# Reading half-filled maxima tiles early, one block's shift rows ahead of other transfers, and LayerNorm statistics joined on GpSimd: one Trainium2 kernel before and after

## The chip, the cores and the metric

The kernel runs on one core of one Trainium2 (trn2) chip. Five engines run their own instruction streams in order and meet through semaphores: PE (TensorE, matrix products), DVE (VectorE), ACT (ScalarE), POOL (GpSimd) and SP (SyncE, which here only issues transfers). The metric is device time in microseconds (us); 35758 instructions are in the trace of one execution.

## The reference, cut to what matters

Input x is (8, 1024, 256); 16 query heads of 16 columns share 4 key and value heads; scores are scaled by 1/16.

```python
n = layernorm(x)
q, k = rope(n @ Wq), rope(n @ Wk)          # 16 heads of q, 4 of k and v
v = n @ Wv
p = softmax(q @ k.T / sqrt(256))           # per head, over 1024 keys
x = x + layernorm((p @ v) @ Wo)
f = layernorm(x) @ (ternary(W) * alpha).T + bias
x = x + layernorm(f)
```

layernorm is (x - mean) / sqrt(var + 1e-5) over 256 columns, without weights.

## The kernel before, in words

**Units and blocks.** The batch is cut into 16 units of 512 queries (`NU`), a unit into 4 blocks (`G`): block i is 512 queries of 4 heads. For each block the score matrix is made twice. One pass (`max_scores`, matmul at L576) has queries on the partitions and 512 keys in the free dimension, and DVE reduces it to the row maximum over the keys (L590). The other (`exp_scores`, L628) has keys on the partitions, and ACT takes its exponential straight into the weights of the value product (L643, then `av_piece`, L663). The maximum reaches the second pass as two extra rows of the query operand `q_st`, which the matmul itself subtracts: DVE splits the maximum into a high and a low part (`shift_split`, L603 and L162, tile `mhl`), PE transposes it (`shift_rows`, L610, tile `pm`), ACT copies it out (L612, `mh`), and SP writes it into rows 48 and 49 of both halves of `q_st` by two transfers (L619). No exponential of a block can be started before its shift rows have landed.

**A maxima tile** (`sm`) is 128 x 2 x 512 fp32 in PSUM, two buffers (`ps_mx`). Two matmuls fill it, one per half (for blocks after the first: both halves of the 1024 keys for one group of rows), and one reduction over both halves (L590, `AX.XY`, 1024 elements to one) empties it. There are 1024 such tiles: 16 of block 0, which keeps its halves apart (`mx_half`, L586, joined at L588), and 1008 of the other blocks.

**The order of the work** is written out by hand for PE, DVE and ACT (`manual_schedule`). It goes by windows: `window` takes three scores of the second pass and, alternating with them, three maxima matmuls that run ahead (`maxima_by`: 40 to 48 matmuls ahead), then whatever `parts_of_step` has for that place (products, transposes, LayerNorm statistics of other units: `Project`, `Tail`), then the value products of a window two back (`av_windows`). A block of 32 scores is ten windows of three and one of two. Three is odd, so every second window of three ends with a maxima tile that is half filled; its second half is the first maxima matmul of the next window.

**GpSimd and SP** are not in that list after the first steps: a planner places their instructions. SP's one queue carries all transfers in the order the planner gives it: inputs, rotated queries out to DRAM and back into `q_st` (`q_to_dram`, L472; `stack_queries`, L542 and the constant rows L146), keys (`kt`, L430; `stack_keys`, L481), the shift rows and the tails' tensors.

**LayerNorm** (`ln_stats`): DVE takes `bn_stats` of each 128 x 256 tile (L237; for each half of the columns a count, a mean and a sum of squared deviations) and joins them by `bn_aggr` (L239); GpSimd adds the epsilon, takes the power -0.5 and negates the mean (L241 to L243).

**The start.** At step numbers below zero only maxima are made; exponentials of block 0 and the projection of units 1 and 2 run side by side. A list at L952 to L978 says which part of which projection comes at which step: `third("kt")` at the thirteenth entry, `stack_queries` of unit 1 at the nineteenth.

Of the kernel before, what the change touches and what calls it, by code (L numbers as in the profile page):

```python
# [8 lines left out]
F32 = mybir.dt.float32  # L9
F32R = mybir.dt.float32r  # L10
AF = mybir.ActivationFunctionType
ALU = mybir.AluOpType
AX = mybir.AxisListType
# [3 lines left out]
P = 128  # L17
# [4 lines left out]
UT = 4  # L22
UQ = UT * P
EPS = 1e-5
# [4 lines left out]
def kernel(  # L29
# [29 lines left out]
    nc = tc.nc  # L59
    B, S, D = x.shape  # L60
# [4 lines left out]
    NK = S // P  # L65
# [9 lines left out]
    small = ctx.enter_context(tc.tile_pool(name="small", bufs=4))  # L75
# [10 lines left out]
    def load_x(u, tag, bufs):  # L86
        b, half = divmod(u, UPB)
        t = xp.tile([P, UT, D], F32, tag=tag, name=f"{tag}_{u}", bufs=bufs)
        src = x[b, half * UQ : (half + 1) * UQ, :].rearrange("(t p) d -> p t d", p=P)
        for ts in (slice(0, 2), slice(2, 4)) if u == 0 else (slice(0, 4),):  # L90
            nc.sync.dma_start(out=t[:, ts, :], in_=src[:, ts, :])
        return t

    x_sb = {0: load_x(0, "x", 2)}
# [4 lines left out]
    mhalf = const.tile([P, 2], F32, name="mhalf")  # L99
# [7 lines left out]
    for src, lo, n in ((w_q, 0, D), (w_k, D, DK), (w_v, ROT, DK)):  # L107
        nc.sync.dma_start(
            out=wqkv[:, :, lo : lo + n], in_=src.rearrange("(c p) n -> p c n", p=P)
# [51 lines left out]
    def split_lo(eng, lo, src, hi):  # L161
        eng.tensor_tensor(lo, src, hi.bitcast(F32), ALU.subtract)  # L162
# [65 lines left out]
        nc.scalar.copy(wt, pt)  # L228


    def ln_stats(src):

        n = src.shape[1]
        mv = small.tile([P, 2, 2], F32, tag="mv", name="mv")[:, :n]
        st = small.tile([P, 2, 6], F32, tag="bnst", name="bnst")
        for t in range(n):
            nc.vector.bn_stats(st[:, t, :], src[:, t, :])  # L237
        for t in range(n):
            nc.vector.bn_aggr(mv[:, t, :], st[:, t, :])  # L239
        sc = small.tile([P, 2, 2], F32, tag="lnsc", name="lnsc")[:, :, :n]  # L240
        nc.gpsimd.tensor_scalar(sc[:, 1, :], mv[:, :, 1], EPS, 1.0, ALU.add, ALU.mult)  # L241
        nc.gpsimd.tensor_tensor(sc[:, 1, :], sc[:, 1, :], mhalf[:, :n], ALU.pow)  # L242
        nc.gpsimd.tensor_scalar(sc[:, 0, :], mv[:, :, 0], -1.0, 0.0, ALU.mult, ALU.add)  # L243
        return mv, sc
# [60 lines left out]
    class Project:  # L305
# [19 lines left out]
                    for p in range(2)  # L325
                ]

        def stats(self, p):
            self.sc[p] = ln_stats(x_sb[self.u][:, 2 * p : 2 * p + 2, :])

        def norm(self, p, eng=None):
            src = x_sb[self.u][:, 2 * p : 2 * p + 2, :]
# [6 lines left out]
            split_lo(eng or self.eng, self.xs[p][1], self.xn[p], self.xs[p][0])  # L339

        def begin(self, p):
            self.stats(p)
            self.norm(p)
            self.hi(p)
            self.lo(p)
# [203 lines left out]
    mx = {}  # L549

    def block_queries(i, r2=slice(None)):

        u, j = divmod(i, G)
        if u < NU - 1:
            return q_st[u % 2][:, j, r2, :]
        return q_st[u % 2][:, :, r2, j * P : (j + 1) * P]

    def max_scores(v):


        i, k = divmod(v // 2, 2 * NK)
        u, part = i // G, v % 2
        if i == 0:
            a, ch, t, r2 = 1 - part, k // NK, k // 2 % UT, k % 2
        else:
            a, ch, t, r2 = 1 - k % 2, part, k // 4, k // 2 % 2
        queries = block_queries(i, r2)
        queries = queries[:, t * P : (t + 1) * P] if u < NU - 1 else queries[:, t]
        if part == 0:
            sm[0] = ps_mx.tile([P, 2, 512], F32, tag="sm", name=f"sm_{i}_{k}")  # L570
            if k == 0:
                mx[i] = small.tile([P, 2, UT, 2], F32, tag="mx", name=f"mx_{i}")
            if k == 0 and i == 0:
                mx["half"] = small.tile([P, 2, 2, UT, 2], F32, tag="mx0", name="mx_half", bufs=1)
        rows = slice(64 * a, 64 * a + 64)
        nc.tensor.matmul(  # L576
            sm[0][:, part, :],
            queries[rows],
            k_st[(u // UPB) % 3][rows, r2, ch * 512 : (ch + 1) * 512],
            start=True,  # L580
            stop=True,
        )
        if part == 0:
            return
        if i == 0:
            nc.vector.tensor_reduce(mx["half"][:, ch, ::-1, t, r2], sm[0], AX.X, ALU.max)  # L586
            if k == 2 * NK - 1:
                nc.vector.tensor_tensor(mx[0], mx["half"][:, 0], mx["half"][:, 1], ALU.max)  # L588
        else:
            nc.vector.tensor_reduce(mx[i][:, a, t, r2 : r2 + 1], sm[0], AX.XY, ALU.max)  # L590
        if k == 2 * NK - 1:
            shift_split(i)
            due.append((v // 4 + (1 if i < 2 else 2), i))

    sm, mhl = {}, {}

    def shift_split(i):

        m = mx.pop(i)
        hl = mhl[i] = small.tile([P, 2, 2, 2 * UT], F32R, tag="mhl", name=f"mhl_{i}")  # L600
        order = "(r t)" if i // G < NU - 1 else "(t r)"
        hi, lo = (hl[:, :, l].rearrange(f"p a {order} -> p a t r", r=2) for l in range(2))
        nc.vector.tensor_copy(hi, m)  # L603
        split_lo(nc.vector, lo, m, hi)

    def shift_rows(i):

        hl = mhl.pop(i)
        pm = psum([8 * UT, P], f"pm_{i}", F32R)
        nc.tensor.transpose(pm, hl.rearrange("p a l x -> p (a l x)"), ident_r)  # L610
        mh = work.tile([8 * UT, P], F32, tag="mh", name=f"mh_{i}")
        nc.scalar.copy(mh, pm.bitcast(F32))  # L612
        n = 4 * UT
        for a in range(2):
            row = 64 * a + NROW
            dst = block_queries(i)[row : row + 2].bitcast(F32)
            if len(dst.shape) == 4:
                dst = dst.rearrange("l j c t -> l (j c) t")
            nc.sync.dma_start(out=dst, in_=mh[n * a : n * a + n, :])  # L619


    es, av_ps, av_sb, d_av = {}, {}, {}, {}
# [64 lines left out]
    class Tail:  # L687
# [85 lines left out]
            ln_apply(self.eng(p), self.on[p], self.x1[p], self.sc[p])  # L773

        def stats_a(self, p):
            self.sc[p] = ln_stats(self.a[p])
            self.add(p)

        def stats_x(self, p):
            self.sc[p] = ln_stats(self.x1[p])  # L780
            self.norm(p)
            self.split(p)

        def stats_f(self, p):
            self.sc[p] = ln_stats(self.a[p])
            self.end(p)

        def ffn(self, p):
# [157 lines left out]
    def second(name, *args):  # L946
        return lambda: getattr(projects[1], name)(*args)

    def third(name, *args):
        return lambda: getattr(projects[2], name)(*args)  # L950

    for k, fs in enumerate((  # L952
        [second("x", 1, 0), second("x", 1, 1), second("kv", 0)],
        [second("kv", 1), (pick, "q", 0, 0, 1), (pick, "q", 0, 1, 1), second("v"),
         second("rotate_k"), second("split_k")],
        [(pick, "q", 1, 0), (keep_warm, 1)],
        [(keep_warm, 3), second("k"), (keep_warm, 4), (pick, "k", 1, 0), (pick, "k", 1, 1),
         (keep_warm, 2)],
        [(pick, "q", 1, 1), second("q_product", 0), third("stats", 0),
         third("norm", 0, nc.scalar)],  # L960
        [second("q_product", 1), third("stats", 1), third("hi", 0, nc.scalar), third("lo", 0),
         (pick, "q", 2, 0)],
        [(pick, "q", 2, 1), third("norm", 1, nc.scalar), third("hi", 1, nc.scalar),
         third("lo", 1), (keep_warm, 3), (fill_constant_parts, 1)],
        [third("x", 0, 0), (pick, "q", 3, 0), (keep_warm, 3)],
        [third("x", 0, 1), (pick, "q", 3, 1), second("rotate_q", 0), (keep_warm, 2)],
        [third("x", 1, 0), third("x", 1, 1), second("split_q", 0)],
        [third("kv_and_dram"), second("rotate_q", 1)],
        [third("v"), second("split_q", 1), second("q_to_dram")],
        [third("kt")],  # L970
        [],
        [(fill_constant_parts, 2)],
        [],
        [third("q", 0)],
        [],
        [third("q", 1), (stack_queries, 1)],
        [third("q_to_dram")],
    )):  # L978
        for f in fs:
            at(k - START, *(f if isinstance(f, tuple) else (f,)))  # L980
# [46 lines left out]
    maxima = [0]  # L1027
# [24 lines left out]
    def window(i, s, size, late):  # L1052
        if done:
            av_out(done.pop())
        if late:
            for r2 in range(2):
                exp_two(s // 4, r2)
        else:
            end = min(maxima_by(s + size), 4 * NSTEP)
            for q in range(max(size, end - maxima[0])):  # L1060
                if q < size:
                    exp_one(s + q)
                if maxima[0] < end:
                    max_scores(maxima[0])
                    maxima[0] += 1
        behind.append((i, s, size))
        for n in range(s // 4, (s + size) // 4):
            parts_of_step(n)
        av_windows(1 if late else 2)
# [135 lines left out]
```

## Time and profile before

| | |
|---|---|
| time, median of 3 runs (lowest to highest) | 1734.97 us (1734.68 to 1735.65) |
| the profiled execution's own time | 1735.28 us |
| its span (first to last instruction) | 1733.1 us |
| busy PE / DVE / ACT / POOL | 92% / 81% / 73% / 48% of the span |
| mean granted TensorE clock | 0.983 of full speed |
| maxima reductions (L590) | 1008, 1218 ns each, 1190.5 us |
| exponentials (L643) | 2000, 602 ns each, 1055.9 us |

How to read it: a busy share says how full an engine is, not that it sets the time; matmuls overlap and are shown busy while they wait, so PE's 92% is no measure of its work. The rows of the waits name who waited for whom, with the total, the count and the longest. In the chain of work that ended last each step is followed back to what released it. A row of a group reads: line, engine, operation, out<-in with its shape, count | busy us, mean ns of one | idle time before it and who ended it.

### The profile page before, as it was taken

Reading aid. Unit: us, or ns where it says so; the run is one execution under the profiler, and the core shown is the slowest. Engines: PE = TensorE matmul, PEld = TensorE weight load, DVE = VectorE, ACT = ScalarE, POOL = GpSimd, SP = SyncE. Lnnn points to the kernel's source line nnn. Section 1 sums busy time; section 2 is a strip of 40 time slices with the busy share of each in tenths; the row PEclk is TensorE's granted clock in tenths of the full one; section 3 lists DMA queues with packets and bytes.
Section 4 is the critical chain, followed back from the end, with each engine's and each line's share of the span. In section 5 each row is a group of like instructions: output and inputs, shape, how many; then the busy total and the mean of one; then the engine's idle time right before and its main releaser. Section 6 shows DMA issues by size and latency. Waiting matters only on the chain.

```text
span 1733.1 us, 35758 instructions
## 1 busy us (share of the span) xinstructions
PE 1602.1 (92%) x14200; PEld 834.1 (48%) x14200; DVE 1398.1 (81%) x1752; ACT 1271.0 (73%) x2479; POOL 836.0 (48%) x1239
## 2 busy tenths in 40 slices
PE   7969999999999999999999999999999999999997
PEld 5534454444544445454454544545454544444444
DVE  6848778888788888878888788888978887888874
ACT  4637777777687777868777777877777786877775
POOL 5522447274453637346374644737455362333354
PEclk8879999999999999999999999999999999999999
DMA  4330424225151332515124151412414141140100
GB/s 131 66 78 32 83 73 87 63 76 97 41 101 43 82 82 61 104 39 98 51 74 96 54 102 46 90 58 78 84 48 95 45 87 51 33 82 32 40 14 25
DMA packets 86071, 117.88 MB, mean 68 GB/s; under 512 B 12089, under 2 KB 50809, under 8 KB 85753
## 3 DMA queue, kind: packets, MB, share of 16 engines
q1 hardware_dynamic: 85904, 115.60, 28.9%
q8 instruction: 112, 1.84, 0.5%
q14 instruction: 55, 0.44, 0.1%
HBM read 68.65 MB, written 45.88 MB: 66 GB/s over the span
## 4 chain that ended last, share of the span: by engine, by line
PE 34%; DVE 13%; POOL 4%; ACT 4%; issue 1%; DMA 1%; SPq 0%; POOLq 0%; ACTq 0%; DVEq 0%
PE av L663 13%; DVE mx L590 10%; PE se L628 10%; PE sm L576 4%; ACT e L643 3%; PE pa L283 2%; PE pf L283 1%; PE pq L283 1%; PE pt_ot L267 1%; DMA dq<-hlq 1%; DVE bnst L237 1%; PE pkv L283 1%; PE pt_xt L267 1%; POOL hlq L162 1%; DVE mhl L603 0%
## 5 line engine op out<-in xcount | busy, mean ns | idle before, releaser
L590 DVE TENSOR_REDUCE mx<-sm 128x1 f32<-128x1024 f32 x1008 | 1190.5, 1218 | 285.5 <-PE sm L576 242.2
L643 ACT ACTIVATE e<-se 128x512 f32<-128x512 f32 x2000 | 1055.9, 602 | 301.3 <-PE sm L576 238.5
L576 PE MATMUL sm<-k_st,q_st 64*128 64x512 f32 x2048 | 736.2, 449 | 45.7 <-DVE mx L590 41.8
L628 PE MATMUL se<-q_st,k_st 64*128 64x512 f32 x2048 | 685.8, 434 | 19.3 <-DMA q_st<-mh 18.3
L663 PE MATMUL av<-e,v_aug 128*32 128x256 f32 (+3 forms) x8096 | 591.7, 392 | 0.0
L628 PEld LDWEIGHTS se<-q_st,k_st 64*128 64x128 f32 x2048 | 330.8, 186 | 368.3 <-ACT e L643 217.3
L576 PEld LDWEIGHTS sm<-k_st,q_st 64*128 64x128 f32 x2048 | 324.5, 186 | 156.7 <-DVE mx L590 125.0
L663 PEld LDWEIGHTS av<-e,v_aug 128*32 128x32 f32 x8096 | 184.3, 109 | 192.6 <-issue 145.7
L241 POOL TENSOR_SCALAR lnsc<-mv 128x2 f32<-128x2 f32 (+1 forms) x134 | 25.8, 193 | 453.6 <-DVE mv L239 448.7
L737 POOL TENSOR_TENSOR xn<-xn,a 128x512 f32<-128x512 f32 x30 | 38.4, 1280 | 129.0 <-DMA a<-d_rec 115.1
L798 POOL TENSOR_TENSOR a<-a,bias_bc 128x512 f32<-128x512 f32 x30 | 39.0, 1300 | 117.2 <-ACT a L797 117.2
L242 POOL TENSOR_TENSOR lnsc<-lnsc,mhalf 128x2 f32<-128x2 f32 (+1 forms) x134 | 92.9, 694 | 0.9
L162 POOL TENSOR_TENSOR hl<-xn,hl 128x512 fp32r<-128x512 f32 x60 | 76.4, 1285 | 0.5
L253 POOL TENSOR_SCALAR xn<-x,lnsc 128x256 f32<-128x256 f32 x116 | 64.9, 568 | 3.4
L297 POOL TENSOR_TENSOR t<-q_rot,sin_q_sb 128x512 f32<-128x512 f32 x31 | 39.7, 1282 | 32.1 <-ACT q_rot L439 32.1
L764 ACT COPY a<-pa 128x512 f32<-128x512 f32 x30 | 17.6, 586 | 45.6 <-issue 45.6
L283 PE MATMUL pq<-xt,wqkvh 128*128 128x256 f32 x256 | 46.1, 304 | 2.8 <-ACT e L643 2.8
L237 DVE BATCH_NORM_STATS2 bnst<-a 128x6 f32<-128x256 f32 x120 | 44.6, 413 | 4.7 <-POOL a L798 4.7
L283 PE MATMUL pa<-woh,hl 128*128 128x256 f32 x240 | 47.0, 298 | 0.2 <-ACT e L643 0.2
L237 DVE BATCH_NORM_STATS2 bnst<-x 128x6 f32<-128x256 f32 x124 | 45.9, 412 | 1.1 <-DMA x<-in_L_attn_x 1.1
L267 PE MATMUL pt_xt<-ident_r,xs 128*128 128x128 f32 x256 | 33.4, 260 | 12.7 <-ACT e L643 11.1
L283 PEld LDWEIGHTS pq<-xt,wqkvh 128*128 128x128 f32 x256 | 36.3, 197 | 14.6 <-ACT e L643 13.2
(156 smaller groups left out, 1320.0 us busy)
## 6 DMA issues: line engine op xcount, KB each, us to landing
q_st<-dq SPq DMA_DIRECT2D x90, 256.0 KB
dq<-hlq SPq DMA_DIRECT2D x60, 256.0 KB
d_av<-avsb SPq DMA_DIRECT2D x60, 256.0 KB
x<-in_L_attn_x SPq DMA_DIRECT2D x15, 512.0 KB
xn<-d_av SPq DMA_DIRECT2D x30, 256.0 KB
a<-d_rec SPq DMA_DIRECT2D x30, 256.0 KB
xr<-in_L_attn_x SPq DMA_DIRECT2D x15, 512.0 KB
out_x<-a SPq DMA_DIRECT2D x30, 256.0 KB
```

The source lines that it names most:

```text
L162: eng.tensor_tensor(lo, src, hi.bitcast(F32), ALU.subtract)
L237: nc.vector.bn_stats(st[:, t, :], src[:, t, :])
L242: nc.gpsimd.tensor_tensor(sc[:, 1, :], sc[:, 1, :], mhalf[:, :n], ALU.pow)
L253: eng.tensor_scalar(dst[:, t, :], src[:, t, :], sc[:, 0, t : t + 1] if eng is nc.gpsimd else mv[:, t, 0:1], sc[:, 1, t : t + 1], ALU.add i ...
L267: nc.tensor.transpose(pt[:, c, t * P : (t + 1) * P], src[:, t, c * P : (c + 1) * P], ident_r)
L283: nc.tensor.matmul(out, chunk(left[i], c), chunk(right[j], c), start=(k == 0), stop=(k == len(steps) - 1),)
L297: eng.tensor_tensor(dst, x, table.unsqueeze(1).to_broadcast(list(x.shape)), ALU.mult)
L576: nc.tensor.matmul(sm[0][:, part, :], queries[rows], k_st[(u // UPB) % 3][rows, r2, ch * 512 : (ch + 1) * 512], start=True, stop=True,)
L590: nc.vector.tensor_reduce(mx[i][:, a, t, r2 : r2 + 1], sm[0], AX.XY, ALU.max)
L628: nc.tensor.matmul(sc if len(queries.shape) == 2 else sc.rearrange("p (j t) -> p j t", j=G), k_st[(i // G // UPB) % 3][rows, r2, kt * P : ...
L643: nc.scalar.activation(e, sc, AF.Exp, scale=1.0 / D**0.5)
L663: nc.tensor.matmul(av_ps[0][32 * r : 32 * r + 32, lo:hi], va[:, kt, r, :], es[i * NK + kt, r // 2, r % 2][:, lo:hi], start=(kt == 0 and lo ...
```

## The change

Three edits, in one diff:

1. A maxima tile of blocks 1 to 63 is no longer reduced to one number per row but to one per half (`AX.X`), into a tile `mx` with a place for each half. At the end of a window that leaves a tile half filled (`reduce_early`), the filled half is reduced by itself; the other half is reduced after it is filled. The halves are joined once per block (`shift_split`, tile `mc`). Block 0 uses the same tile.
2. `kt` of the third projection and `stack_queries` of unit 1 are called under `tc.issue_after(shifts[1])`, which makes the planner issue their transfers after the shift rows of block 1; `kt` moves from the thirteenth to the eighteenth entry of the list.
3. Where LayerNorm is applied by GpSimd, GpSimd also joins the two halves of the `bn_stats` result, in eight instructions of 128 x 2 elements (128 x 1 in the last tail), and DVE's `bn_aggr` falls away. Statistics of the first three projections and of the last tail's parts on DVE stay as they were.

```diff
+    def join_stats(neg_mean, rstd, st):
+        eng, (m0, m1), (s0, s1) = nc.gpsimd, (st[:, 1, i] for i in range(2)), (
+            st[:, 2, i] for i in range(2)
+        )
+        eng.tensor_tensor(neg_mean, m0, m1, ALU.add)
+        eng.tensor_scalar(neg_mean, neg_mean, -0.5, 0.0, ALU.mult, ALU.add)
+        eng.tensor_tensor(s0, s0, s1, ALU.add)
+        eng.tensor_scalar(s0, s0, 1.0 / D, EPS, ALU.mult, ALU.add)
+        eng.tensor_tensor(m0, m0, neg_mean, ALU.add)
+        eng.tensor_tensor(m0, m0, m0, ALU.mult)
+        eng.tensor_tensor(rstd, s0, m0, ALU.add)
+        eng.tensor_tensor(rstd, rstd, mhalf[:, : rstd.shape[1]], ALU.pow)
...
-    def ln_stats(src):
+    def ln_stats(src, joined_by=None):
...
+        if joined_by is nc.gpsimd:
+            join_stats(sc[:, 0, :], sc[:, 1, :], st[:, :n].rearrange("p t (i k) -> p k i t", i=2))
+            return None, sc
...
         def begin(self, p):
-            self.stats(p)
+            self.stats(p, nc.gpsimd)
...
-            self.sc[p] = ln_stats(self.a[p])
+            self.sc[p] = ln_stats(self.a[p], self.eng(p))
...
         if i == 0:
-            nc.vector.tensor_reduce(mx["half"][:, ch, ::-1, t, r2], sm[0], AX.X, ALU.max)
-            if k == 2 * NK - 1:
-                nc.vector.tensor_tensor(mx[0], mx["half"][:, 0], mx["half"][:, 1], ALU.max)
+            nc.vector.tensor_reduce(mx[i][:, ch, ::-1, t, r2], sm[0], AX.X, ALU.max)
         else:
-            nc.vector.tensor_reduce(mx[i][:, a, t, r2 : r2 + 1], sm[0], AX.XY, ALU.max)
+            reduce_halves(i, k, 2)
...
+    def reduce_halves(i, k, n):
+        lo = len(reduced)
+        a, t, r2 = 1 - k % 2, k // 4, k // 2 % 2
+        nc.vector.tensor_reduce(mx[i][:, lo:n, a, t, r2], sm[0][:, lo:n, :], AX.X, ALU.max)
+        reduced.extend(range(lo, n))
+
+    def reduce_early(v):
+        i, k = divmod(v // 2, 2 * NK)
+        if i > 0 and v % 2:
+            reduce_halves(i, k, 1)
...
     def shift_split(i):
-        m = mx.pop(i)
+        halves = mx.pop(i)
+        m = small.tile([P, 2, UT, 2], F32, tag="mc", name=f"mc_{i}")
+        nc.vector.tensor_tensor(m, halves[:, 0], halves[:, 1], ALU.max)
...
-            nc.sync.dma_start(out=dst, in_=mh[n * a : n * a + n, :])
+            shifts[i] = nc.sync.dma_start(out=dst, in_=mh[n * a : n * a + n, :]).ins
...
+    def behind_shift(i, f, *args):
+        with tc.issue_after(shifts[i]):
+            f(*args)
...
-        [third("kt")],
+        [],
         [],
         [(fill_constant_parts, 2)],
         [],
         [third("q", 0)],
-        [],
-        [third("q", 1), (stack_queries, 1)],
+        [(behind_shift, 1, third("kt"))],
+        [third("q", 1), (behind_shift, 1, stack_queries, 1)],
         [third("q_to_dram")],
...
                     maxima[0] += 1
+            reduce_early(maxima[0])
         behind.append((i, s, size))
```

## The prediction

> **What bounds the kernel now.** I read the page first: busy shares and the chain of work that ended last.
>
> ```profile
> PE 1602.1 (92%) x14200; PEld 834.1 (48%) x14200; DVE 1398.1 (81%) x1752; ACT 1271.0 (73%) x2479; POOL 836.0 (48%) x1239
> PE 34%; DVE 13%; POOL 4%; ACT 4%; issue 1%; DMA 1%; SPq 0%; POOLq 0%; ACTq 0%; DVEq 0%
> L590 DVE TENSOR_REDUCE mx<-sm 128x1 f32<-128x1024 f32 x1008 | 1190.5, 1218 | 285.5 <-PE sm L576 242.2
> ```
>
> No engine is full, yet the second largest owner of the chain is DVE, nearly all of it the maxima reduction. DVE also stood idle 285 us before those reductions, mostly for the matmul that fills the tile. So PE and DVE wait for each other. The table of waits gives the sizes (total, times, longest):
>
> ```profile
> DVE mx L590 <- PE sm L576: 242.2, 339, 14.0
> PEld sm L576 <- DVE mx L590: 125.0, 204, 2.3
> PE sm L576 <- DVE mx L590: 41.8, 119, 1.8
> PE se L628 <- DMA q_st<-mh: 18.3, 8, 13.0
> ```
>
> The weight load (PEld) waits where the matmul will; an earlier matmul still draining hides part, so PE's idle 41.8 us understates the loss. The chain over two typical windows shows the mechanism (start, us, what):
>
> ```profile
> 1141.45 2.37 DVE mx L590 x2
> 1143.82 0.04 issue
> 1143.86 0.49 PE sm L576
> 1144.35 0.78 PE av L663 x8
> 1145.13 0.42 PE se L628
> 1145.55 0.05 PE sm L576
> 1145.60 0.02 issue
> 1145.63 2.37 DVE mx L590 x2
> ```
>
> It is a ring of 4.18 us per two windows (1141.45 to 1145.63): two reductions (B, begun when the window's first matmul filled it, then C), then the next window's third maxima matmul, which waits for C's buffer and leaves its own tile half filled, then the value products, then the matmul that fills that tile. While PE does the value products DVE has only one tile to reduce and then idles (0.69 us before 1145.63).
>
> How often: in the timeline there are 310 three-score windows that begin on an empty tile and 309 that begin on a half-filled one. Where no other work follows, the first last 2.04 us on average (247 windows), the second 1.75 (157); undisturbed ones of either kind last 1.68. In an undisturbed window the third maxima matmul starts 0.57 us after the first score matmul. Summed over the windows on an empty tile after 108 us, it starts 100 us later than that: 111 windows are late by 0.7 us or more, most of the rest by under 0.2.
>
> At the start a second loss stands in SP's queue and PE's row:
>
> ```profile
> 84.44 3.07 SPq L430 DMA_DIRECT2D dk<-ks  x4
> 90.07 3.30 SPq L481 DMA_DIRECT2D k_st<-dk  x6
> 93.42 2.30 SPq L542 DMA_DIRECT2D q_st<-dq  x5
> 96.23 1.41 SPq L619 DMA_DIRECT2D q_st<-mh  x2
> 105.85 0.94 PE L628 MATMUL se<-q_st,k_st 64*128 64x512 f32 x2 [13.01 <-DMA q_st<-mh]
> ```
>
> The shift rows of block 1 were ready at 87.45 (end of ACT's copy), stood behind the last of these 15 issues until 96.23, and landed behind the five query loads of 256 KB each.
>
> **What the Trainium skill says.** *PSUM — Partial Sum Buffer*, "PSUM bank collisions raise a hardware error": an engine may read one bank while TensorE writes another; a bank is 512 fp32, here one half of a tile. No row of before shows a half read while the other is written. *TensorE: Matmul & The Clock Gate*, "What's actually happening": an idle window of some 3.4 us halves TensorE's clock. The trace agrees: clock 0.50 over 105.85 to 118.3, after the 13 us stall. *GPSIMD Engine Reference*, "1. Specifications": GpSimd and VectorE contend for SBUF when VectorE has two SBUF inputs or a two-port mode. The trace agrees: the 128x16 cast at L603 takes 0.18 us at the median, 1.13 at 640.25 beside GpSimd's 128x512 subtraction, 1.28 at most.
>
> **The change part by part.** The built program has PE's order unchanged and ACT's but for one copy at the end; DVE has 313 split tiles.
>
> *Half reads.* A full reduction takes 1.22 us alone and 1.13 queued (3.49 us for three). The one 512-element reduction (L203) took 0.68; queued I take 0.59, the same 0.09 less. So a split costs 2 x 0.59 - 1.13 = 0.05 us of DVE, 313 x 0.05 = 16 us. On the ring, B leaves only its second half: 0.59 + 1.24 in place of 2.37, so the pair goes from 4.18 to 3.64. PE's own pair is 1.68 + 1.68 to 1.84, ACT's six exponentials 3.25 (649.06), DVE's 2 x 1.13 + 2 x 0.59 = 3.44: all fit under 3.64. Each late third matmul gains the smaller of its lateness and 0.54: over the windows on an empty tile, **77 us**. Ends: 20 us if queues refill at once, 115 if nearly all lateness goes (the second kind of window, too, is late by some 30 us).
>
> *The join per block*: 63 more 128x16 operations on DVE, at L162's 336 ns: 21 us, between a block's last reduction and its split. Half lies in DVE's idle time, half on the ring: **10 us** lost (0 to 21).
>
> *Joining on GpSimd*: DVE loses 235 joins; a pair took 0.30 us at 654.84, so 35 us. They stand in windows with extra PE work: I count **4 us** gained (0 to 15). GpSimd gets 119 x 5 = 595 more small instructions. Two-input 128x512 takes 1285 ns and 128x256 735, so 128x2 about 190; with the 0.27 us pitch of dependent ones (1083.30 to 1083.57), a join takes 1.3 us more. GpSimd goes to about 60% busy. Cover: the closest consumers are the transposes of the tail's split, 4.4 us after their source (1103.56 against 1099.18), DVE's `bn_stats` of L798's sum, 4.2, and of L769's, 3.0 at least. GpSimd's new order puts the queries' split ahead of the tail's normalization, so the tail's high part is 2 to 3 us later; with PE also about 1 us earlier that cover is just used up. I take **4 us** lost (0 to 20). In the last tail nothing covers: the chain passes three joins (1689.29, 1696.21, 1701.20), each 1.3 longer less 0.2 of DVE's: **3.5 us** lost.
>
> *DVE's splits* where DVE itself is behind: **5 us** lost of the 16.
>
> *The shift rows.* SP issues block 1's two right after the copy: 87.5 to 88.9. Uncrowded ones reach PE about 2 us after issue (1190.51 to 1192.6), so at 91, ahead of PE's need at 92.84: **13 us** gained (10 to 13). The stretch at half clock held 12 us of PE work; at full clock it would lose up to 6, and DVE and ACT hold it back: **3.5 us** gained (0 to 6). What is now late: 4 key writes, 6 key loads, 6 query loads and 2 constant rows, 18 issues. Unit 1's queries land near 108 and are first read at 151.6 by block 4's maxima; the keys of batch 1 are first read at 254.5. If neither lay so far off, the 13 us would come back.
>
> *What is late next* in each unit: kv product, `d_k` out (2.3 us), in again (4.4), GpSimd's rotation (3.7), four writes, six loads, and behind them on SP the shift rows that PE needs at once (issued 1190.51, PE waited 0.39 at 1192.61; at 269.7, 373.6, 476.9 and 579.8 it waited 0.8 to 1.3). This is latency; PE gains about 0.8 us across it, so 14 x 0.8 = **11 us** given back.
>
> Sum: -77 + 10 - 4 + 4 + 5 + 11 = -51 in the steady part, -16.5 at the start, +3.5 at the end: -64. The profiled execution took 1735.28 (span 1733.1 and 2.2 around it), so 1671.3; the median of the runs is 0.3 lower: **1671**.
>
> **The rivals.** *DVE becomes the bound.* If half reads don't overlap in the queue they cost 0.68 each: 313 x 0.23 = 72 us more, DVE's pair is 3.62 with no room for statistics or the join, and every backlog falls on PE; about 25 of the 51 stay: 1697. For: the spare time is thin. Against: full reads overlap by 0.09. *The half reads do nothing*, since PE's next wait ends at the same moment (ACT's score buffers, three of them): 16.5 - 3.5 = 13 gained, 1722. Against: ACT has 4% of the chain and 3.25 us in a 3.64 us pair. *Nearly all lateness goes*: 115 in place of 77, and little given back: 1630. *Slower*: GpSimd's burst (1078.15 to 1105.36, unbroken) gets three joins, 3.9 us; the queries' split is in it, SP's four writes of the queries wait for it (1201.11 to 1205.82), and the next block's shift rows stand behind them (1211.15, so 5.3 us spare). It decides when the burst is late by over 5.3 us; to eat the 64 us it must be late by 5.3 + 64/14 = 10 us; at 10.7 the time is 1741. Against: the new order has the split earlier in the burst. That the change doesn't do what it says is excluded: the instructions are in the program.
>
> **How the numbers follow.** Chances: forecast 0.55 (its own range 1650 to 1690), DVE the bound 0.22, start alone 0.08, nearly all 0.06, slower 0.08, no difference 0.01. Range 1645 to 1710: the first two with their ends; the rest is left out. About 0.2% can be told from no change: faster 0.91, same 0.01, slower 0.08.
>
> **What would show it.** Right: pairs near 3.64 us; the third matmul late by under 30 us in sum; DVE's idle time before reductions down by over 60; no 13 us stall before block 1 and full clock after it; waits on `q_st<-mh` longer in other blocks. Wrong: half reads above 0.7 us; PE's waits for DVE unchanged; transposes waiting for GpSimd; shift rows still landing late because the query writes before them fill the DMA engines.

## The result, and the profile after

The changed kernel takes 1825.25 us (median of 4 runs, 1821.95 to 1828.95), the kernel before 1734.83 (4 runs): ratio 1.0532, 95% interval 1.0496 to 1.0568. It is 90 us slower where 64 us of gain were forecast. The profiled execution took 1826.66 us, its span 1824.5.

The page of the changed kernel, busy shares and the chain's owners:

```profile
PE 1652.5 (91%) x14200; PEld 843.0 (46%) x14200; DVE 1408.9 (77%) x1893; ACT 1297.8 (71%) x2479; POOL 940.9 (52%) x1834
...
PE 21%; DVE 13%; ACT 2%; POOL 2%; issue 1%; POOLq 0%; ACTq 0%
```

Its groups of instructions by line and shape (busy us, mean ns, then idle time before them and who ended it), full reads and half reads of a maxima tile:

```profile
L613 DVE TENSOR_REDUCE mx<-sm 128x2 f32<-128x1024 f32 x695 | 839.4, 1219 | 156.4 <-PE sm L592 128.7 <-PE se L657 16.7
L613 DVE TENSOR_REDUCE mx<-sm 128x1 f32<-128x512 f32 x626 | 429.5, 686 | 205.6 <-PE sm L592 203.3 <-PE se L657 2.1
```

DVE works hardly more than before (1408.9 against 1398.1 us) and is less full. So it is not a fuller DVE that took the time. What grew are the waits of both engines for each other (total, times, longest):

```profile
DVE mx L613 <- PE sm L592: 331.9, 435, 3.2
...
PEld sm L592 <- DVE mx L613: 239.9, 381, 2.6
...
PE sm L592 <- DVE mx L613: 114.4, 239, 2.2
```

Before, these three rows were 242.2, 125.0 and 41.8 us. The chain of work over one pair of windows (start, us, what) shows where:

```profile
1104.24 0.72 PE se L657 x2
1104.96 0.02 issue
1104.98 1.83 DVE mx L613 x2
1106.82 0.04 issue
1106.86 0.50 PE sm L592 x2
1107.37 0.46 PE se L657 x2
```

And the timeline of the same stretch (start, us, engine, what, idle time before it and who ended it):

```profile
1104.98 1.82 DVE L613 TENSOR_REDUCE mx<-sm 128x2 f32<-128x1024 f32 x2 [1.35 <-PE se L657]
...
1105.08 0.86 PE L692 MATMUL av<-e,v_aug 128*32 128x256 f32 x16
...
1105.87 0.50 PE L657 MATMUL se<-q_st,k_st 64*128 64x512 f32 x1
...
1106.86 0.50 PE L592 MATMUL sm<-k_st,q_st 64*128 64x512 f32 x2 [0.50 <-DVE mx L613]
```

From 1104.98 DVE reads a full tile and then, queued behind it, the first half of the half-filled tile, until 1106.81. The next window's first score starts at 1105.87, and its first maxima matmul, which fills the second half of that tile, should stand right behind it. It starts at 1106.86: when DVE has read the first half. The other two scores and the value products are behind it in PE's order.

The built program says the same. A matmul that fills a second half waits for DVE in 313 of 1024 cases, in the program before in none; the 313 are the split tiles. One of them, in the words of the program's semaphores (DVE adds one per instruction):

```
PE   sm_32_9, columns 0 to 511     waits for DVE >= 946
DVE  read of columns 0 to 511      brings DVE to 950
PE   sm_32_9, columns 512 to 1023  waits for DVE >= 950
```

The two halves have no word in common, but the program orders the write to a tile behind an unfinished read of the same tile.

Counted over the three-score windows after 108 us that begin on a half-filled tile, the window's first maxima matmul starts 0.71 us after the first score on average (303 windows; 0.01 before), later than 0.5 us in 245. On the windows that begin on an empty tile, the lateness that I wanted to remove did fall: the time by which the third maxima matmul starts later than the undisturbed 0.57 us went from 121 to 65 us in sum, and the windows in which it is late by 0.7 or more from 111 to 31. Windows without other work show the exchange in their mean length: 2.04 to 1.88 us on an empty tile, but 1.75 to 2.45 on a half-filled one.

At the start the stall of 13 us is gone; SP's queue puts the shift rows first:

```profile
88.28 1.41 SPq L648 DMA_DIRECT2D q_st<-mh  x2
89.78 2.35 SPq L447 DMA_DIRECT2D dk<-ks  x4
93.18 2.94 SPq L498 DMA_DIRECT2D k_st<-dk  x5
```

### The profile page after: what moved, and what is told of

The parts are those of the page before. It is cut to its first block, busy times and chain, and to the rows that moved or that the text cites. A ratio compares the mean times of both kernels' runs of the same rounds, so it can differ in the third digit from the quotient of the medians.

```text
span 1824.5 us, 36485 instructions
## 1 busy us (share of the span) xinstructions
PE 1652.5 (91%) x14200; PEld 843.0 (46%) x14200; DVE 1408.9 (77%) x1893; ACT 1297.8 (71%) x2479; POOL 940.9 (52%) x1834
## 5 line engine op out<-in xcount | busy, mean ns | idle before, releaser
L613 DVE TENSOR_REDUCE mx<-sm 128x1 f32<-128x512 f32 (+1 forms) x1321 | 1221.9, 966 | 361.9 <-PE sm L592 331.9
L672 ACT ACTIVATE e<-se 128x512 f32<-128x512 f32 x2000 | 1082.5, 601 | 377.2 <-PE sm L592 254.7
L592 PE MATMUL sm<-k_st,q_st 64*128 64x512 f32 x2048 | 648.2, 453 | 118.1 <-DVE mx L613 114.4
L657 PE MATMUL se<-q_st,k_st 64*128 64x512 f32 x2048 | 703.9, 431 | 2.0 <-ACT e L682 1.0
L657 PEld LDWEIGHTS se<-q_st,k_st 64*128 64x128 f32 x2048 | 343.1, 186 | 366.2 <-ACT e L672 243.6
L592 PEld LDWEIGHTS sm<-k_st,q_st 64*128 64x128 f32 x2048 | 281.0, 186 | 256.2 <-DVE mx L613 239.9
L236 POOL TENSOR_TENSOR lnsc<-bnst 128x2 f32<-128x2 f32 (+1 forms) x119 | 23.4, 197 | 406.3 <-DVE bnst L250 406.3
L243 POOL TENSOR_TENSOR lnsc<-lnsc,mhalf 128x2 f32<-128x2 f32 (+1 forms) x119 | 83.2, 700 | 9.1
L284 PE MATMUL pt_ot<-ident_r,hl 128*128 128x128 f32 x240 | 31.0, 253 | 13.1 <-ACT e L672 10.2
```

The source lines that it names most:

```text
L243: eng.tensor_tensor(rstd, rstd, mhalf[:, : rstd.shape[1]], ALU.pow)
L284: nc.tensor.transpose(pt[:, c, t * P : (t + 1) * P], src[:, t, c * P : (c + 1) * P], ident_r)
L592: nc.tensor.matmul(sm[0][:, part, :], queries[rows], k_st[(u // UPB) % 3][rows, r2, ch * 512 : (ch + 1) * 512], start=True, stop=True,)
L613: nc.vector.tensor_reduce(mx[i][:, lo:n, a, t, r2], sm[0][:, lo:n, :], AX.X, ALU.max)
L657: nc.tensor.matmul(sc if len(queries.shape) == 2 else sc.rearrange("p (j t) -> p j t", j=G), k_st[(i // G // UPB) % 3][rows, r2, kt * P : ...
L672: nc.scalar.activation(e, sc, AF.Exp, scale=1.0 / D**0.5)
```

## The experiments

My theory **W**: the loss is the wait of the second half's matmul on the early read, and PE's order behind it. Rivals: **D**, DVE's extra work; **J**, the GpSimd joins or the reordered transfers. All kernels compute the full result. Ratios are to the kernel before, run on the same chip.

**Whole tiles.** The changed kernel with the early read taken out:

```diff
-            reduce_early(maxima[0])
```

> The changed kernel without the early read: every maxima tile is reduced once, when both halves are full; shift rows, join of the halves per block and GpSimd joins stay. Theory W (the early read makes the matmul that fills the second half wait until DVE has read the first, and PE's order behind it): the whole loss goes, 1715 to 1735 us, PE's waits for DVE before maxima back to some 120 of about 42 us in all, and 125 for the weight loads. Rival J (the GpSimd joins or the reordered transfers cost the time): stays above 1790.

Measured: 1763.29 us, ratio 1.0158 (1.0126 to 1.0189). The early read accounts for 62 us of the 90, but W is not all: 28 us of loss remain, where I expected 0 to 20 of gain. The lengths of the windows show the two sides of the early read. From the 21st window on, the same 303 three-score windows that begin on an empty tile last 758.8 us in all with whole tiles and 662.3 with the early read, 97 less; the same 302 that begin on a half-filled tile last 667.2 and 828.1, 161 more.

**The same halves, read late.** Split tiles are noted instead of read, and both reads come when the tile is full:

```diff
         else:
+            if in_two and in_two.pop() == (i, k):
+                reduce_halves(i, k, 1)
             reduce_halves(i, k, 2)
...
-            reduce_halves(i, k, 1)
+            in_two.append((i, k))
```

> The same 313 tiles are read in two halves, but both reads come when the tile is full, so DVE has the work of the changed kernel and PE has no new wait. W: 0.05 to 0.15 us per split tile on DVE, partly hidden, so 5 to 30 us above the run with whole tiles: 1725 to 1760. Rival D (DVE's extra work is the loss): about the changed kernel's 1825, 1800 at least.

Measured: 1761.55 us, ratio 1.0147 (1.0093 to 1.0200), the same as with whole tiles within the noise, and just above the range that I gave. DVE's maxima work did rise, from 1191.8 to 1211.0 us by the pages' rows, 0.06 us per split, but no cost of it shows in the time. D falls: the same halves, read when the tile is full, are free of the loss.

**Each half a tile of its own.** Four tiles of 512 in place of two of 1024, each reduced straight after its matmul, so every read is early and no matmul waits for a read of its own tile:

```diff
-ps_mx = ctx.enter_context(tc.tile_pool(name="ps_mx", bufs=2, space=PSUM))
+ps_mx = ctx.enter_context(tc.tile_pool(name="ps_mx", bufs=4, space=PSUM))
...
-        if part == 0:
-            sm[0] = ps_mx.tile([P, 2, 512], F32, tag="sm", name=f"sm_{i}_{k}")
+        half = ps_mx.tile([P, 512], F32, tag="sm", name=f"sm_{i}_{k}_{part}")
...
-            sm[0][:, part, :],
+            half,
...
+        nc.vector.tensor_reduce(mx[i][:, ch, a, t, r2 : r2 + 1], half, AX.X, ALU.max)
```

> Each half is its own tile (four of 512 instead of two of 1024), reduced by itself straight after its matmul: 2048 half reads, no matmul waits for a read of its own tile's other half. W: the wait of PE's third matmul and of the second half go; DVE's maxima work is 2048 x 0.59 to 0.68 = 1210 to 1390 us against 1269 in the changed kernel; 1680 to 1745. D: DVE has more work than in the changed kernel, so 1825 or more.

Measured: 1680.38 us, ratio 0.9694 (0.9657 to 0.9731). Its reductions, and then its waits:

```profile
L597 DVE TENSOR_REDUCE mx<-sm 128x1 f32<-128x512 f32 x2048 | 1252.3, 679 | 180.6 <-PE sm L590 161.1 <-PE se L652 18.7
```

```profile
PEld sm L590 <- DVE mx L597: 66.9, 112, 2.8
...
PE sm L590 <- DVE mx L597: 28.8, 31, 2.4
```

PE's waits for DVE are down to a quarter of those of the changed kernel (28.8 against 114.4 us), although DVE's reductions take 12 us more (1252.3 against 1221.9 by the page's row for L613 and 18.7 for block 0's). Against whole tiles, with the same joins and transfers, that is 83 us, and by the lengths of the same windows nearly all of it lies where the early read was meant to help: 84 us in those that begin on an empty tile, 2 in the others. So an early place in DVE's queue is not what cost the changed kernel its time; the wait is. What the 313 early reads alone would win without the wait is not shown, because here every tile is read and freed by halves, not only those at the windows' ends.

**The second half one score later**, in the changed kernel, in windows that begin on a half-filled tile:

```diff
+            ahead = 1 if size == 3 and maxima[0] % 2 else 0
             for q in range(max(size, end - maxima[0])):
-                if q < size:
-                    exp_one(s + q)
+                for k in range(q + ahead if q else 0, q + ahead + 1):
+                    if k < size:
+                        exp_one(s + k)
```

> The changed kernel, but in a window that begins on a half-filled tile two scores instead of one stand ahead of the matmul that fills the second half, so it comes 0.28 us later in PE's order. W: each of some 310 windows wins most of 0.28 us, 50 to 90 us: 1735 to 1775, and PE's waits for DVE before maxima fall from 114 to under 70 us. D: within 10 us of 1825.

Measured: 1799.83 us, ratio 1.0373 (1.0344 to 1.0401): 25 us won, not 50 to 90. PE's waits did not fall (127.8 after 114.4 us), and the matmul still starts 0.74 us after the window's first score: moved one score back, it still waits for the end of the read. What is won is the score that is no longer behind it. The windows that begin on a half-filled tile are 66 us shorter in all (828.1 to 761.9), as W says, but those on an empty tile are 38 longer (662.3 to 700.6); why they lose was not followed up.

**The edits, each alone on the kernel before.** Edit 2:

```diff
-        [third("kt")],
+        [],
...
-        [],
-        [third("q", 1), (stack_queries, 1)],
+        [(behind_shift, 1, third("kt"))],
+        [third("q", 1), (behind_shift, 1, stack_queries, 1)],
```

> The kernel before with the second edit alone (key and query transfers of the start issued behind the shift rows of block 1). Prediction's step: 13 us and some of 3.5 us gained, 1717 to 1724, no stall of PE on q_st<-mh at 93 us. Rival Q (the transfers that are now later hold something up, and are part of the 28 us that the changed kernel without early reads loses to the kernel before): 1735 to 1755.

Measured: 1721.37 us, ratio 0.9934 (0.9913 to 0.9954): 11 us gained. Rival Q falls. Edit 3:

```diff
-            self.sc[p] = ln_stats(self.a[p])
+            self.sc[p] = ln_stats(self.a[p], self.eng(p))
```

> The kernel before with the third edit alone (GpSimd joins the LayerNorm statistics). Theory M (the 28 us are the join of the halves per block on DVE, 64 x 0.42 us, beside GpSimd's long instructions): 1731 to 1745. Rival J (GpSimd's eight small instructions per join are late for what follows): 1755 to 1780, with PE or DVE waiting for GpSimd.

Measured: 1752.63 us, ratio 1.0105 (1.0062 to 1.0149): 18 us lost, between the two expectations. Edit 1:

```diff
-            nc.vector.tensor_reduce(mx[i][:, a, t, r2 : r2 + 1], sm[0], AX.XY, ALU.max)
+            reduce_halves(i, k, 2)
...
+            reduce_early(maxima[0])
```

> The kernel before with the first edit alone (early reads and the join per block). Theory W (the matmul of the second half waits for the early read): it has the whole loss and none of the gain at the start, 1830 to 1850. If edits 2 and 3 were part of the loss it would be under 1815.

Measured: 1835.19 us, ratio 1.0591 (1.0557 to 1.0624). As W says, edit 1 has the whole loss. Edit 1 without its last line, so that only the join per block is left of it:

```diff
-            reduce_early(maxima[0])
```

> The kernel before with tiles of all blocks reduced at once to one number per half and these joined once per block (63 more operations of 128x16 on DVE, ahead of the split of the maxima); no early read, no other edit. M: 63 x 0.28 to 0.42 us, and stalls of PE for DVE behind them, 18 to 40 us above before: 1753 to 1775. J: 0 to 10 us above, 1735 to 1745.

Measured: 1749.11 us, ratio 1.0093 (1.0063 to 1.0123): 16 us lost, again between the two expectations. Within their intervals the parts add up: -11 + 18 + 16 is 23 us, and whole tiles lost 28.

**Why the joins cost anything.** The timeline of the kernel with whole tiles at one of its long stalls (DVE and POOL, then PE's wait at the end):

```profile
421.21 0.52 DVE L628 TENSOR_TENSOR mc<-mx 128x16 f32<-128x16 f32 x1
...
421.68 2.50 POOL L162 TENSOR_TENSOR hl<-xn,hl 128x512 fp32r<-128x512 f32 x2
421.77 1.23 DVE L632 CAST mhl<-mc 128x16 fp32r<-128x16 f32 x1
...
423.04 1.19 DVE L162 TENSOR_TENSOR mhl<-mc,mhl 128x16 fp32r<-128x16 f32 x1
424.14 2.34 DVE L613 TENSOR_REDUCE mx<-sm 128x2 f32<-128x1024 f32 x2
...
425.41 0.79 PE L592 MATMUL sm<-k_st,q_st 64*128 64x512 f32 x1 [2.54 <-DVE mx L613]
```

Three DVE operations of 128x16 elements, some 0.18 us each by themselves, take 2.94 us beside GpSimd's two-input operations, and the reductions behind them are late for PE. In the kernel with joins on GpSimd alone, the cast and the subtraction take 33.8 and 28.2 us, before 21.0 and 21.5: 19.5 us more, about as much as that kernel lost. GpSimd's instructions meet more of the splits there: 25 of the 64 casts take over 0.6 us, 9 before. Of the 30 casts over 0.3 us, 27 run beside a two-input operation of GpSimd of 128 or more columns (for over 0.3 of their time), of the 34 shorter ones 2. The Trainium skill names the condition (*GPSIMD Engine Reference*, "1. Specifications": GpSimd's SBUF interfaces are shared with VectorE and contended when VectorE has two SBUF inputs or is in a two-port mode), and *VectorE: DVE Perf Modes*, "The perf-mode tier table", lists a copy of fp32 in SBUF at 2x and `tensor_reduce` at 1x only. No run here shows the mode that the cast ran in. That gives a test: the same cast as a reduction over an axis of one, in the kernel with edit 3 alone.

```diff
-        nc.vector.tensor_copy(hi, m)
+        one = m.rearrange("p a t (r o) -> p a t r o", o=1)
+        nc.vector.tensor_reduce(hi, one, AX.X, ALU.max)
```

> The kernel with GpSimd joins alone, but the cast of the maxima's high part (128x16 fp32, 33.8 us in all there, 25 of 64 over 0.6 us beside GpSimd's two-input operations, 21.0 us and 9 in the kernel before) is a reduction over an axis of one, the form that no trace shows stretched. Theory C (the joins' 20 us are DVE's small copies and subtractions stretched beside GpSimd): no cast over 0.6 us, and 10 to 20 us of the 20 are won, 1732 to 1745; the subtraction behind it can still be stretched. Rival J (late GpSimd results hold PE or DVE): 1748 to 1757, as with the cast.

Measured: 1721.73 us, ratio 0.9947 (0.9930 to 0.9965): by the ratios 27 us won by one form of one small instruction, more than C gave. The instructions on the tile `mhl` (ns: shortest, median, longest), with the cast and then with the reduction:

```profile
L620 DVE CAST mhl<-mx x64: 174/186/1337, 55.8 to 1697.6; 128x16 fp32r<-128x16 f32 x64
L162 DVE TENSOR_TENSOR mhl<-mx,mhl x64: 175/189/1224, 56.7 to 1697.8; 128x16 fp32r<-128x16 f32 x64
```

```profile
L621 DVE TENSOR_REDUCE mhl<-mx x64: 170/182/190, 55.3 to 1662.5; 128x16 fp32r<-128x16 f32 x64
L162 DVE TENSOR_TENSOR mhl<-mx,mhl x64: 174/318/1292, 55.5 to 1662.7; 128x16 fp32r<-128x16 f32 x64
```

None of the 64 reductions is stretched, although 29 of them run beside such an operation of GpSimd, as 29 of the casts did; the two-input subtraction still is, as the condition in the Trainium skill has it. The rival that GpSimd's late results hold PE or DVE falls: GpSimd makes the same joins here. The cast took 22.1 us less (33.8 to 11.7), the gain is a little more, and the kernel with the joins in it is now 9 us faster than before. What the new form of the cast alone would bring to the kernel before was not run.

**Even windows.** On edit 2 alone, four and two maxima matmuls by turns, so no window leaves a half-filled tile:

```diff
             end = min(maxima_by(s + size), 4 * NSTEP)
+            end += end % 2
```

> Shift rows first, tiles read whole, but windows take four and two maxima matmuls by turns instead of three and three, so no tile is left half filled at a window's end. If the half-filled tile at the border is what the kernel before loses in its ring, some 40 to 80 us under the run with the shift rows alone (1721): 1640 to 1680. If the loss is only DVE's two reductions in a row against PE's need of the buffer, the four matmuls of one window wait as long: 1715 to 1745.

Measured: 1695.91 us, ratio 0.9806 (0.9761 to 0.9851), 25 us under edit 2 alone: less than I expected of it, more than its rival gave.

**Half tiles without GpSimd joins, and then with reductions.** The first is the kernel with half tiles and LayerNorm joined as before; the second replaces the join per block and the cast:

> Separate half tiles and shift rows first, LayerNorm joined by DVE as in the kernel before (no GpSimd joins). If the parts add up as for whole tiles, the 1680 of the half tiles less the 20 of the joins: 1655 to 1668. If DVE, then 86% busy, is the bound there, the joins on DVE (35 us of work) cost as much as they win: 1675 to 1690.

Measured: 1677.48 us, ratio 0.9704 (0.9673 to 0.9736), within the noise of the 1680 with joins. The 18 us of the joins don't appear here. The number lies in the range of the second case, in which DVE's own joins cost as much as they win; whether that is the reason, or fewer splits meet GpSimd's long operations, the runs don't separate.

```diff
-        nc.vector.tensor_tensor(m, halves[:, 0], halves[:, 1], ALU.max)
+        pairs = halves.rearrange("p h a t r -> p a t r h")
+        nc.vector.tensor_reduce(m, pairs, AX.X, ALU.max)
...
-        nc.vector.tensor_copy(hi, m)
+        nc.vector.tensor_reduce(hi, pairs, AX.X, ALU.max)
```

> As the run with half tiles and DVE joins of LayerNorm, but the join of the halves per block and the high part of the split are reductions over an axis of two instead of an elementwise maximum and a copy. C: neither is over 0.6 us any more, 15 to 25 us of DVE work and a part of it on the path: 5 to 15 us under that run. Without C: within 4 us of it.

Measured: **1646.78 us**, ratio 0.9509 (0.9488 to 0.9530): 31 us under the run above where C gave 5 to 15, and the fastest of all, 4.9% faster than the kernel before. The groups of the three small operations in the run above, then the same in this one, and then PE's waits for transfers and for DVE in this one:

```profile
L162 DVE TENSOR_TENSOR mhl<-mc,mhl 128x16 fp32r<-128x16 f32 x64 | 24.6, 384 | 2.2
L627 DVE CAST mhl<-mc 128x16 fp32r<-128x16 f32 x64 | 24.3, 380 | 2.2
L623 DVE TENSOR_TENSOR mc<-mx 128x16 f32<-128x16 f32 x64 | 17.9, 279 | 2.2
```

```profile
L162 DVE TENSOR_TENSOR mhl<-mc,mhl 128x16 fp32r<-128x16 f32 x64 | 19.8, 310 | 2.2
L624 DVE TENSOR_REDUCE mc<-mx 128x16 f32<-128x32 f32 x64 | 12.0, 188 | 2.2
L628 DVE TENSOR_REDUCE mhl<-mx 128x16 fp32r<-128x32 f32 x64 | 11.4, 179 | 0.0
```

```profile
PE se L653 <- DMA q_st<-mh: 19.8, 12, 3.8
...
PE sm L590 <- DVE mx L597: 4.4, 12, 1.0
```

PE's direct wait for DVE before maxima is down from 41.8 us in the kernel before to 4.4; the largest single row of PE's own waits is now the shift rows.

## Why the prediction was wrong, point by point

**Half reads (-77), the step that failed.** I worked out the ring with B's remaining half "0.59 + 1.24 in place of 2.37", and let PE fill the second half whenever it came to it. The Trainium skill allows that for two banks (*PSUM — Partial Sum Buffer*, "PSUM bank collisions raise a hardware error"), and I wrote beside it that "no row of before shows a half read while the other is written", but went on as if the program would do it. I compared the order of instructions on each engine, not the waits, and so the wait of the second half's matmul for the half read stands at nothing in the sum. In the program that matmul waits, and the half read stands behind a full one: 0.71 us per window on average, in some 300 windows. Measured: about 62 us lost in the changed kernel (against whole tiles) and 86 alone (edit 1 alone less edit 1 without early reads), not 77 gained. The windows on a half-filled tile pay 161 us for the wait in both pairs of kernels. The benefit side was about right: the windows on an empty tile win 97 us in the first pair and 70 in the second. Their lateness before was 121 us by the count used here, not the 100 of the prediction; the 77 hardly depends on it (78 by this count).

**The durations were right.** A half read took 686 ns on average (I had 0.68 alone), a full one 1219, and queued 1.82 us for both (0.59 + 1.24 is 1.83). A split costs DVE 0.06 us with late halves (I had 0.05), and none of it shows in the time (+5 forecast).

**The join per block (+10, 0 to 21)**: 16 us (11 to 21). Its 305 to 443 ns fit the 336 that I took, but I priced it alone, not the later reads behind it.

**Joins on GpSimd (about +3.5 in all)**: 18 us alone. I looked for transposes waiting for GpSimd; PE's waits for POOL before `pt_xt` and `pt_ot` are only 5.6 us in all in the kernel with edit 3 alone, 2.0 before. I had myself quoted the cast of 1.13 us beside GpSimd and the Trainium skill's sentence on contention, and then put the stretching that joins on GpSimd would add at nothing in the sum. The form of the cast alone wins 27 us back. The join's own price held (small GpSimd instructions 192 to 201 ns, I had 190).

**Shift rows (-13 and -3.5)**: 11 us gained (8 to 15). In the changed kernel they are issued at 88.28 in place of 96.23, the stall is gone, and PE waits for none of the transfers that were moved behind them. So the first term came about. The second did not: with edit 2 alone the clock is again 0.50 from 112 to 120 us, although PE by that trace is never idle for longer than 0.99 us between 84 and 120. The idle window of 3.4 us that the prediction names as the cause is not there in that trace; what brings the half clock there stays open.

**The shift rows' chain (+11 given back)**: not isolated. In the changed kernel PE is too slow for it to show; in the fastest kernel PE waits 19.8 us for `q_st<-mh` in 12 places, without a stall of 13 us at the start, which fits a loss of that kind and size but doesn't prove it.

**The rivals.** "DVE the bound" needed a fuller DVE; it was at 77%. The slower rival had the right sign (at 10.7 us its own sum gives 1747, not the 1741 that stands there), but its mechanism (queries' split, SP, shift rows) did not occur: the shift rows were not waited for. "That the change doesn't do what it says is excluded: the instructions are in the program" was the wrong test. The instructions were there; the overlap that they were for was not. None of my cases put a chance on a new wait inside the very tile that was split.

## What to carry to other kernels

To read part of a buffer early can cost more than it wins if the program orders writes behind reads by whole tiles (here 161 us against 97): give the parts tiles of their own, and check the waits of the instruction that fills the other part, not only the order. Before a wait is removed from one engine, ask what the earlier instruction stands behind in its own queue, for its end is what the new wait is for. Small copies on DVE that others wait for should not meet GpSimd's long two-input operations; where they must, use a form that the trace does not show stretched.

## What the runs showed of the hardware that I had not expected

A 128x16 copy or maximum on DVE takes 0.18 us, or up to 1.34 beside GpSimd; the same copy as a reduction took 170 to 190 ns in all 64 cases, 29 of them beside a two-input operation of GpSimd. Changing the form gained 27 us in one kernel (the cast alone) and 31 in another (1677.48 to 1646.78, the join as well). In the second the three small operations took 66.8 us before and 43.2 after, 24 less; where the remaining 7 come from was not separated.
